# Leaving out the padding columns in layers 2 and 3 of a four-layer graph network

## The chip, the cores and the metric

The kernel runs on one core of one Trainium2 chip. The metric is the device time of one execution in microseconds. Before the change the median of three runs is 1538.35 us (1538.09 to 1540.38).

## The reference

A graph of 3125 nodes with 128 features each and 103,125 directed edges (100,000 drawn, 3125 loops) goes through four graph layers, each with a residual and a layer norm. The change touches the third and the fourth, called layer 2 and layer 3 (counting from 0):

```python
# layer 2: attention along the edges
e = jnp.sum(Q[receiver] * K[sender], axis=-1) * scale
w = jnp.exp(e - m[receiver])
denom = jax.ops.segment_sum(w, receiver, num_segments=num_nodes)
numer = jax.ops.segment_sum(w[:, None] * V[sender], receiver, num_segments=num_nodes)
return x + attn @ Wo           # attn = numer / denom

# layer 3: two rounds of "mean over the neighbours, then two matrices"
x = _sage_conv(features, src, dst, w1_l, b1, w1_r)
x = jax.nn.relu(x)
x = _sage_conv(x, src, dst, w2_l, b2, w2_r)
return jax.nn.sigmoid(x)
```

## The kernel before, in words

**Tiling.** Nodes come in NB = 25 blocks of P = 128, so NP = 3200 columns stand for N = 3125 nodes; the last 75 columns are padding. The edges are turned once, at the start, into a dense matrix of edge counts (bf16, in HBM, `f_ctd`): 25 blocks of 128 sources by 3200 targets. All later layers are dense products against it. A padding node has no edges, so its counts are zero.

**Layer 2** (L1339 to L1448) takes the targets in two groups, `QG`: 13 blocks (1664 columns) and 12 blocks (1536 columns). For each group it walks the 25 source blocks; a pair (group, source block) is an item. `scores` (L1364) loads the item's counts (`ct2`, L1368), and for chunks of m columns multiplies the turned features `xT` with `yT` into a PSUM bank `s` (L1373), takes the exponential on ScalarE (L1376) and multiplies by the counts on VectorE (L1377), which leaves the edge weights in the tile `e2`. m is 416 in the first group (four chunks) and 512 in the second (three). `products2` (L1381) then uses each 128-column block of `e2` as weights and streams 129 columns of values and ones, adding up over the source blocks in PSUM. In program order the scores of item i+1 stand before the products of item i; `ct2` and `e2` have three buffers each, the banks `s` three. `turned_y` (L1345) makes `yT` in steps of 512 columns; the three steps for the second group are put between items near the end of the first (L1423).

**Layer 3** (L1451 on) starts with `add1` (L1473): for each of 25 source blocks, and for each bank of at most 512 columns in `CH` (six of 512 and one of 128), three bf16 parts of the features (`ips`) are the weights and the counts `ct3` are streamed, summing in seven PSUM banks. The last five source blocks are kept and added bank by bank, and in that loop (L1529) each finished bank is scaled by the degrees (`aT`, L1534), goes through the hidden layer (`hidden`, L1505 to L1507, f32 products of the bank's width, Relu into `uT`), and then block by block through `around` and `own` (both by `second`, L1513), which read `uT` in blocks of 128 columns as weights. The second aggregation, `add2` (L1549), uses the counts as weights.

**What orders the work.** [...] Inside layer 2 the order of the item loop is written out in the source. The framework that builds the program adds the waits and may put independent instructions of an engine in another order than the source's: in layer 3 some products of L1549 stand between those of L1513. GpSimd has no work in the second group and in layer 3.

Of the kernel before, what the change touches and what calls it, by code (L numbers as in the profile page):

```python
# [7 lines left out]
F32 = mybir.dt.float32  # L8
# [7 lines left out]
P = 128  # L16
N = 3125
NB = 25
NP = NB * P
# [7 lines left out]
CH = [(c, min(512, NP - c)) for c in range(0, NP, 512)]  # L27
# [472 lines left out]
GM = 40.0  # L500
IG = [(0, 4), (4, 7), (11, 7), (18, 7)]
QG = [(0, 13), (13, 12)]


@with_exitstack
def fast_path(
# [4 lines left out]
    nc = tc.nc  # L511
# [3 lines left out]
    ctd = dram.tile([NB, P, NP], BF16, name="f_ctd")  # L515
# [13 lines left out]
    def copy(o, i):  # L529
        rr[0] ^= 1  # L530
        if rr[0]:
            nc.scalar.copy(o, i)
        else:
            nc.vector.tensor_copy(o, i)
# [317 lines left out]
    for b in range(NBT):  # L852
# [5 lines left out]
        for k in range(0, BW, 4):  # L858
            cp = cps.tile([P, 4, P], F32, name="cp", tag="cw")
            wp = cps.tile([P, 4, P], F32, name="wp", tag="cw")  # L860
            for j in range(4):
                for q in range(2):
                    w = q * BW + k + j
# [4 lines left out]
            for j in range(4):  # L868
                for q in range(2):
                    w = q * BW + k + j  # L870
# [5 lines left out]
            i0 = (b % SB) * BW * WN + k * WN  # L876
# [9 lines left out]
        if b % SB == SB - 1:  # L886
            i0 = (b - SB + 1) * BW * WN
# [30 lines left out]
    nq = lp.tile([P, NB], F32, name="nq")  # L918
    nm = lp.tile([P, len(QG)], F32, name="f_nm")
    due = []  # L920
# [7 lines left out]
    def step():  # L928

        todo = [f for k, f in due if k <= now[0]]  # L930
        due[:] = [(k, f) for k, f in due if k > now[0]]
        for f in todo:
            f()
        now[0] += 1

    def bank():
        return spare[-1]()
# [56 lines left out]
    def bound2(sp, q):  # L994

        i0, n = QG[q]
        mq = sp.tile([P, 1], F32, name="mq")
# [11 lines left out]
    def finish1(sp, g, gap):  # L1009
# [26 lines left out]
        def turns(j):  # L1036
# [5 lines left out]
            else:  # L1042
                nc.gpsimd.tensor_tensor(xs, xs, xs, OP.add)
                for q, (a, m) in enumerate(QG):
                    if i0 < a + m <= i0 + n:
# [4 lines left out]
    with ExitStack() as st:  # L1050
# [238 lines left out]
        acc = None  # L1289
        for x_, (g, hp, c) in enumerate(items):  # L1290
            i0, n = IG[g]
            if (g, hp, c) == (1, 0, 0):
                zero.close()
                ap = st.enter_context(tc.tile_pool(name="f_ap1", bufs=1, space=PSUM))
                spare.append(lambda: ap.tile([P, 512], F32, name="few"))
            if c == 0:
                if g == 0:
                    acc = [zps.tile([P, 512], F32, name="acc1", tag=f"acc{3 + k}") for k in range(2)]
                    acc += [zpp.tile([P, 512], F32, name="acc1", tag=f"left{k}") for k in range(2)]
                else:  # L1300
                    acc = [ap.tile([P, 512], F32, name=f"acc1_{k}") for k in range(n)]
# [32 lines left out]
    with ExitStack() as st:  # L1334
# [4 lines left out]
        ap = st.enter_context(tc.tile_pool(name="f_ap2", bufs=1, space=PSUM))  # L1339
# [3 lines left out]
        def turned_y(a, n):  # L1343
            t = bank()
            nc.tensor.matmul(t[:, :n], wyv[:, 0:P], xT[:, a : a + n], start=True, stop=True)  # L1345
            copy(yT[:, a : a + n], t[:, :n])
# [12 lines left out]

        items = [(q, c) for q in range(len(QG)) for c in range(NB)]  # L1360
        es = {}
        split = QG[1][0] * P

        def scores(q, c):  # L1364
            i0, n = QG[q]
            w = n * P
            ct = cp.tile([P, 13 * P], BF16, name="ct2")
            nc.sync.dma_start(ct[:, :w], ctd[c, :, i0 * P : (i0 + n) * P])  # L1368
            e = cp.tile([P, 13 * P], F32, name="e2")
            m = 416 if w % 416 == 0 else 512  # L1370
            for a in range(0, w, m):
                s = ss.tile([P, 512], F32, name="s")
                nc.tensor.matmul(  # L1373
                    s[:, :m], xT[:, c * P : (c + 1) * P], yT[:, i0 * P + a : i0 * P + a + m], start=True, stop=True
                )
                nc.scalar.activation(e[:, a : a + m], s[:, :m], AF.Exp, bias=nm[:, q : q + 1], scale=scale)  # L1376
                nc.vector.tensor_tensor(e[:, a : a + m], e[:, a : a + m], ct[:, a : a + m], OP.mult)  # L1377
            es[q, c] = e
# [31 lines left out]
        for a in range(0, split, 512):  # L1410
            turned_y(a, min(512, split - a))
        scores(*items[0])
        acc = None
        for x_, (q, c) in enumerate(items):
            i0, n = QG[q]
            if c == 0:
                acc = [ap.tile([P, 512], F32, name=f"acc2_{k}") for k in range((n + 2) // 3)]
            step()
            if (q, c) == (0, 3):
                degrees()  # L1420
            if q == 0 and NB - 4 <= c < NB - 1:
                a = split + (c - NB + 4) * 512
                turned_y(a, min(512, NP - a))  # L1423
            if x_ + 1 < len(items):
                scores(*items[x_ + 1])
            if c < NB - 2:
                for k in range(n):
                    products2(acc, q, c, k)
            elif c == NB - 1:
                for k0 in range(0, n, 3):  # L1430
                    m = min(3, n - k0)
                    for b in (NB - 2, NB - 1):
                        for k in range(k0, k0 + m):
                            products2(acc, q, b, k)
                for k0 in range(0, n, 3):
                    m = min(3, n - k0)
                    t = acc[k0 // 3][:, 0 : m * (P + 1)].rearrange("p (b d) -> p b d", d=P + 1)
                    z = cp.tile([P, 3], F32, name="z2")
                    nc.vector.tensor_scalar(z[:, 0:m], t[:, :, P], 1e-38, None, OP.max)
                    nc.vector.reciprocal(z[:, 0:m], z[:, 0:m])  # L1440
                    for j in range(m):
                        b = i0 + k0 + j
                        nc.vector.scalar_tensor_tensor(
                            r[:, b, :], t[:, j, 0:P], z[:, j : j + 1], x[:, b, :], OP.mult, OP.add
                        )
                finish2(q)
# [5 lines left out]
    with ExitStack() as st:  # L1452
# [4 lines left out]
        ap = st.enter_context(tc.tile_pool(name="f_ap3", bufs=1, space=PSUM))  # L1457
        aT = fp.tile([P, NP], F32, name="f_aT")
        uT = fp.tile([P, 2, NP], F32, name="f_uT")
        v = vo[:, :, 0:P]  # L1460
        for g in range(3, len(GB)):
            b0, n = GB[g]
            ips[g] = in_parts(lp, g, x[:, b0 : b0 + n, :])

        def counts(b):
            ct = cp.tile([P, NP], BF16, name="ct3")
            nc.sync.dma_start(ct, ctd[b])
            return ct


        acc = [ap.tile([P, 512], F32, name=f"acc3_{k}") for k in range(len(CH))]

        def add1(ct, b, k):  # L1473
            c, n = CH[k]
            for s in range(3):
                nc.tensor.matmul(  # L1476
                    acc[k][:, :n], ips[b // 4][:, b % 4, s, :], ct[:, c : c + n], start=(b == 0 and s == 0),
                    stop=(b == NB - 1 and s == 2),
                )

        for b in range(NB - HB):
            ct = counts(b)
            for k in range(len(CH)):
                add1(ct, b, k)
            if 3 <= b < 17 and b % 2:
                turned(ps, xT, *GB[(b - 3) // 2])
            if b == 18:

                sd = fp.tile([P, 1], F32, name="f_sumdeg")
                nc.vector.tensor_reduce(sd, deg, AX.X, OP.add)  # L1490
                t = ps.tile([P, 512], F32, name="tr")
                nc.tensor.matmul(t[:, 0:1], ones, sd, start=True, stop=True)
                nc.vector.tensor_scalar(good[:, 2:3], t[:, 0:1], float(E), None, OP.is_equal)
                nc.vector.tensor_tensor(good[:, 3:4], good[:, 0:1], good[:, 1:2], OP.mult)
                nc.vector.tensor_tensor(good[:, 3:4], good[:, 3:4], good[:, 2:3], OP.mult)
                nc.vector.tensor_copy(flag, good[0:1, 3:4])
# [2 lines left out]

        def hidden(k):  # L1500

            c, n = CH[k]
            for f in range(2):
                t = ap.tile([P, 512], F32, name=f"acc3_{k}") if f == 0 else ps.tile([P, 512], F32, name="tr")
                nc.tensor.matmul(t[:, :n], w1l[:, f * P : (f + 1) * P], aT[:, c : c + n], start=True, stop=False)  # L1505
                nc.tensor.matmul(t[:, :n], w1r[:, f * P : (f + 1) * P], xT[:, c : c + n], start=False, stop=True)
                nc.scalar.activation(uT[:, f, c : c + n], t[:, :n], AF.Relu, bias=b1[:, f : f + 1])  # L1507
# [17 lines left out]
            t = second(ps.tile([P, 512], F32, name="tr"), g, w2r)  # L1525
            nc.vector.tensor_tensor(v[:, b0 : b0 + n, :], t, b2[:, None, :].to_broadcast([P, n, P]), OP.add)

        K = len(CH)
        for k in range(K + 3):  # L1529
            if k < K:  # L1530
                for b in range(NB - HB, NB):
                    add1(last[b], b, k)
                c, n = CH[k]
                nc.vector.tensor_tensor(aT[:, c : c + n], acc[k][:, :n], rdr[:, c : c + n], OP.mult)  # L1534
            if 0 <= k - 1 < K:
                hidden(k - 1)
            if 0 <= k - 2 < K:
                around(k - 2)
            if 0 <= k - 3 < K:
                own(k - 3)  # L1540


        acc = [ap.tile([P, 4, P], F32, name=f"acc3_{g}") for g in range(len(GB))]
# [11 lines left out]
        for b in range(NB - HB):  # L1555
            ct = counts(b)
# [3 lines left out]
        for g, (b0, n) in enumerate(GB):  # L1560
# [10 lines left out]
            m = min(n, NF - b0)  # L1571
# [48 lines left out]
```

## Time and profile before

The execution that was profiled took 1536.56 us.

| | us |
|---|---|
| median of three runs | 1538.35 |
| profiled execution | 1536.56 |
| its span, first to last instruction | 1534.5 |
| TensorE busy in the span | 1400.5 |
| layer 2, second group (25 items) | about 1120 to 1255 |
| layer 3, first aggregation and hidden layer | 1261.7 to about 1412 |
| layer 3, second aggregation on TensorE | 1412.6 to 1505.2 |

In the costliest groups of the page, each line gives the source line, engine and operation, the tiles and shapes, the count, then busy time and mean ns of one, then the idle time before it:

```profile
L1377 DVE TENSOR_TENSOR e<-e,ct 128x416 f32<-128x416 f32 (+1 forms) x175 | 110.4, 636 | 108.2 <-ACT e L1376 102.6
L1376 ACT ACTIVATE e<-s,f_nm 128x416 f32<-128x416 f32 (+1 forms) x175 | 111.5, 642 | 99.4 <-PE s L1373 94.1
L1373 PE MATMUL s<-yT,f_xT 128*128 128x416 f32 (+1 forms) x350 | 145.8, 552 | 4.6 <-ACT rt L1356 4.0
L1381 PE MATMUL acc<-self__8127,e 128*128 128x129 f32 x1250 | 148.7, 276 | 0.6 <-DVE e L1377 0.6
L1476 PE MATMUL acc<-ct,ip 128*128 128x512 bf16 (+1 forms) x525 | 104.9, 360 | 1.4 <-DMA ct<-f_ctd 1.4
```

An f32 product is recorded as two matmuls. A matmul's record begins before its predecessor ends, since they are pipelined; the mean of one (552 ns) is therefore longer than the step from one to the next. The step is read from the chain of waits, where each piece covers only the time that it adds.

### The profile page before, as it was taken

The numbers are of one execution on the slowest core, as the hardware profiler recorded it, in microseconds if no ns is written. First come the engines' busy times: TensorE is split into PE (matmuls) and PEld (weight loads), VectorE is DVE, ScalarE is ACT, GpSimd is POOL, SyncE is SP. The second block draws the span as 40 slices with busy tenths as digits, with TensorE's granted clock in tenths as the row PEclk, the third lists the DMA queues.
The fourth block names the chain that finished last, engine by engine and source line by source line (L and its number), as shares of the span: only waits on it lengthen the run. The fifth ranks groups of instructions, "written<-read, shape, count | busy, mean of one in ns | idle before, by whom it ended". The sixth has DMA issues, their size and how long they took to land.

```text
span 1534.5 us, 35155 instructions
## 1 busy us (share of the span) xinstructions
PE 1400.5 (91%) x14871; PEld 1223.6 (80%) x14871; DVE 981.0 (64%) x1574; ACT 923.4 (60%) x1880; POOL 122.5 (8%) x136
## 2 busy tenths in 40 slices
PE   4899999999997978899989989899999989999995
PEld 3898999998997867899979889577777764458995
DVE  4999899989991389778878887544464360012005
ACT  2988778888882489878778676544474340023006
POOL 1000000000000023203311320300000000000000
PEclk9999999999999999999999999999999999999998
DMA  6387787878877623444434333332222226513551
GB/s 192 91 220 207 203 234 206 235 202 223 214 214 232 222 85 101 143 118 125 132 115 134 114 87 95 106 94 68 67 72 73 82 105 238 193 44 129 195 195 45
DMA packets 210368, 224.39 MB, mean 146 GB/s; under 512 B 72892, under 2 KB 184007, under 8 KB 209945
## 3 DMA queue, kind: packets, MB, share of 16 engines
q1 hardware_dynamic: 206344, 217.74, 48.4%
q10 hardware_dynamic: 3457, 2.35, 0.6%
q8 instruction: 118, 1.93, 0.5%
q0 software_dynamic: 400, 1.97, 0.4%
q14 instruction: 49, 0.40, 0.1%
HBM read 157.67 MB, written 64.36 MB: 145 GB/s over the span
## 4 chain that ended last, share of the span: by engine, by line
PE 40%; DVE 5%; ACT 2%; issue 1%; POOL 1%; DMA 1%; DVEq 0%; ACTq 0%; SPq 0%; POOLq 0%
PE acc L1381 9%; PE s L1373 8%; PE acc L1476 7%; PE acc L1549 6%; PE acc L1241 4%; PE acc L1236 2%; DVE cm L1226 1%; DVE nz L1260 1%; PE tr L1513 1%; PE acc L1513 1%; DMA ct<-f_ctd 1%; ACT fm L1225 1%; DVE cm L1219 0%; PE tr L1505 0%; PE acc L1505 0%
## 5 line engine op out<-in xcount | busy, mean ns | idle before, releaser
L1241 PE MATMUL acc<-vp,cm 128*128 128x198 bf16 x2500 | 344.7, 252 | 6.6 <-DVE cm L1226 4.1
L1225 ACT ACTIVATE fm<-adr,bas 128x896 bf16<-128x896 f32 (+1 forms) x320 | 286.5, 952 | 68.0 <-DVE cm L1226 63.1
L1236 PE MATMUL acc<-vp,ct 128*128 128x204 bf16 x1250 | 315.2, 256 | 10.0 <-DVE vp L1144 5.6
L1241 PEld LDWEIGHTS <-cm 128*128 128x128 bf16 x2500 | 236.0, 98 | 26.5 <-issue 10.6
L872 PE MATMUL wp<-wod,ohc 128*128 128x128 bf16 x3840 | 244.0, 219 | 8.8 <-ACT cs L877 6.6
L872 PEld LDWEIGHTS <-ohc 128*128 128x128 bf16 x3840 | 224.0, 98 | 9.8 <-issue 9.4
L833 DVE TENSOR_TENSOR wod<-ohd,w 128x4096 bf16<-128x4096 bf16 (+1 forms) x120 | 225.0, 1931 | 0.6 <-PE wp L872 0.6
L1226 DVE TENSOR_TENSOR cm<-fm,ct 128x896 bf16<-128x896 bf16 (+1 forms) x320 | 198.1, 649 | 36.1 <-PE acc L1241 14.1
L842 ACT ACTIVATE wod<-ohd,wu 128x128 bf16<-128x128 bf16 x640 | 197.0, 400 | 0.0
L1377 DVE TENSOR_TENSOR e<-e,ct 128x416 f32<-128x416 f32 (+1 forms) x175 | 110.4, 636 | 108.2 <-ACT e L1376 102.6
L1376 ACT ACTIVATE e<-s,f_nm 128x416 f32<-128x416 f32 (+1 forms) x175 | 111.5, 642 | 99.4 <-PE s L1373 94.1
L1381 PEld LDWEIGHTS acc<-self__8127,e 128*128 128x128 f32 x1250 | 148.4, 193 | 21.5 <-issue 19.7
L1373 PE MATMUL s<-yT,f_xT 128*128 128x416 f32 (+1 forms) x350 | 145.8, 552 | 4.6 <-ACT rt L1356 4.0
L1381 PE MATMUL acc<-self__8127,e 128*128 128x129 f32 x1250 | 148.7, 276 | 0.6 <-DVE e L1377 0.6
L794 PE MATMUL acc<-f_xw,cw 128*128 128x128 f32 x1000 | 118.4, 278 | 7.4 <-DMA cw<-wd 7.4
L1236 PEld LDWEIGHTS <-ct 128*128 128x128 bf16 x1250 | 122.4, 98 | 2.5 <-issue 1.5
L883 ACT COPY ws<-wp 128x512 f32<-128x512 f32 x160 | 93.6, 585 | 49.8 <-PE wp L872 48.2
L794 PEld LDWEIGHTS acc<-f_xw,cw 128*128 128x128 f32 x1000 | 115.0, 194 | 7.6 <-DMA cw<-wd 7.6
L864 PE MATMUL cp<-ohc,ohd 128*128 128x125 bf16 x1280 | 96.7, 218 | 21.1 <-ACT ws L883 17.9
L1373 PEld LDWEIGHTS s<-yT,f_xT 128*128 128x128 f32 x350 | 62.2, 191 | 57.7 <-issue 40.6
L1476 PE MATMUL acc<-ct,ip 128*128 128x512 bf16 (+1 forms) x525 | 104.9, 360 | 1.4 <-DMA ct<-f_ctd 1.4
L1549 PE MATMUL acc<-ip,ct 128*128 128x128 bf16 x1875 | 105.2, 219 | 0.0
(277 smaller groups left out, 1482.7 us busy)
## 6 DMA issues: line engine op xcount, KB each, us to landing
ct<-f_ctd SPq DMA_DIRECT2D x50, 800.0 KB
wd<-ws SPq DMA_DIRECT2D x40, 896.0 KB
ct<-f_ctd SPq DMA_DIRECT2D x150, 224.0 KB
cw<-wd SPq DMA_DIRECT2D x50, 640.0 KB
f_ctd<-cs SPq DMA_DIRECT2D x20, 1000.0 KB
ct<-f_ctd SPq DMA_DIRECT2D x25, 416.0 KB
ct<-f_ctd SPq DMA_DIRECT2D x25, 384.0 KB
cw<-wd SPq DMA_DIRECT2D x25, 320.0 KB
```

The lines of the kernel that those rows point to most:

```text
L794: nc.tensor.matmul(accs[j // 4][:, j % 4, :], cw[:, j - h, :], xw[:, i, :], start=False, stop=(i == NB - 1 and (j % 4 == 3 or j == n - 1)) ...
L833: nc.vector.tensor_tensor(f[:, 0:n].rearrange("p w (a t) -> p w a t", t=2), ohd[:, 0:n].rearrange("p w (a t) -> p w a t", t=2), twos(w2[s] ...
L842: nc.scalar.activation(wod[2][:, BW + w, :], ohd[:, BW + w, :], AF.Copy, scale=w3[:, 1, at : at + 1])
L872: nc.tensor.matmul(wp[:, j, :], ohc[:, w, :], wod[s][:, w, :], start=(j == 0 and q == 0 and s == 0), stop=(j == 3 and q == 1 and s == 2), ...
L1225: nc.scalar.activation(f[:, : n * P], at, AF.Relu, bias=bas[:, c, h : h + 1], scale=UP)
L1226: nc.vector.tensor_tensor(m[:, : n * P], f[:, : n * P], ct[:, : n * P], OP.min)
L1236: nc.tensor.matmul(out_(F1, PW), ct[:, k * P : (k + 1) * P], vp[:, c, hp : hp + 2, :, 2 * F1 : V1], start=(c == 0), stop=False, skip_group ...
L1241: nc.tensor.matmul(out_(0, 2 * F1)[:, j], ms[j][:, k * P : (k + 1) * P], vp[:, c, hp + j, :, 0 : 2 * F1], start=False, stop=(c == NB - 1 a ...
L1373: nc.tensor.matmul(s[:, :m], xT[:, c * P : (c + 1) * P], yT[:, i0 * P + a : i0 * P + a + m], start=True, stop=True)
L1381: nc.tensor.matmul(acc[k // 3][:, (k % 3) * (P + 1) : (k % 3 + 1) * (P + 1)], es[q, c][:, k * P : (k + 1) * P], vo[:, c, 0 : P + 1], start ...
L1476: nc.tensor.matmul(acc[k][:, :n], ips[b // 4][:, b % 4, s, :], ct[:, c : c + n], start=(b == 0 and s == 0), stop=(b == NB - 1 and s == 2),)
L1549: nc.tensor.matmul(acc[g][:, j, :], ct[:, (b0 + j) * P : (b0 + j + 1) * P], ups[b // 4][:, b % 4, s, :], start=(b == 0 and s == 0 and j == ...
```

## The change

```diff
+LN = N - (NB - 1) * P
+CN = [(c, min(512, N - c)) for c in range(0, N, 512)]
...
         def scores(q, c):
             i0, n = QG[q]
-            w = n * P
+            w = min(n * P, N - i0 * P)
             ct = cp.tile([P, 13 * P], BF16, name="ct2")
-            nc.sync.dma_start(ct[:, :w], ctd[c, :, i0 * P : (i0 + n) * P])
+            nc.sync.dma_start(ct[:, :w], ctd[c, :, i0 * P : i0 * P + w])
             e = cp.tile([P, 13 * P], F32, name="e2")
-            m = 416 if w % 416 == 0 else 512
+            m = w // (4 if q == 0 else 3)
+            assert w % m == 0 and m <= 512
+            if w < n * P:
+                nc.gpsimd.memset(e[:, w : n * P], 0.0)
             for a in range(0, w, m):
...
-                turned_y(a, min(512, NP - a))
+                turned_y(a, min(512, N - a))
...
         uT = fp.tile([P, 2, NP], F32, name="f_uT")
+        nc.gpsimd.memset(uT[:, :, N:], 0.0)
...
-        acc = [ap.tile([P, 512], F32, name=f"acc3_{k}") for k in range(len(CH))]
+        acc = [ap.tile([P, 512], F32, name=f"acc3_{k}") for k in range(len(CN))]
...
         def add1(ct, b, k):
-            c, n = CH[k]
+            c, n = CN[k]
...
         def hidden(k):
-            c, n = CH[k]
+            c, n = CN[k]
...
-        K = len(CH)
+        K = len(CN)
...
-                c, n = CH[k]
+                c, n = CN[k]
                 nc.vector.tensor_tensor(aT[:, c : c + n], acc[k][:, :n], rdr[:, c : c + n], OP.mult)
```

The second group of layer 2 has w = 1461 columns in place of 1536, in three chunks of 487. The 75 columns of `e2` that `products2` still reads as weights are set to zero on GpSimd, in each of the 25 items. The last step of `turned_y` makes 437 columns. In layer 3 `CN` has the same six banks of 512 and a last one of 53, used by `add1`, the scaling and `hidden`; the 75 padding columns of `uT` are set to zero once. Everything that works in blocks of 128 nodes (`products2`, `around`, `own`, `add2`) keeps its shapes, as does the first group of layer 2.

More of the change, by code (lines that the diff above doesn't have):

```diff
@@ L1482, in fast_path @@
             ct = counts(b)
-            for k in range(len(CH)):
+            for k in range(len(CN)):
                 add1(ct, b, k)
```

## The prediction

> **What bounds the kernel now.** I read the page's chain of waits first, then the same chain in order of time in layers 2 and 3, and then stretches with busy times. The chain's shares say that TensorE leads, and that the two lines of layer 2, L1381 and L1373, lead it.
>
> ```profile
> PE 40%; DVE 5%; ACT 2%; issue 1%; POOL 1%; DMA 1%; DVEq 0%; ACTq 0%; SPq 0%; POOLq 0%
> ```
>
> In order of time (start, length, what) the first group alternates between products of 416 columns (eight records an item: each f32 product leaves two) and the second between products of 512 (six records).
>
> ```profile
> 1089.44 2.79 PE s L1373 x8
> 1092.24 2.90 PE acc L1381 x26
> ...
> 1220.90 2.58 PE s L1373 x6
> 1223.48 2.68 PE acc L1381 x24
> 1226.16 2.58 PE s L1373 x6
> 1228.73 2.68 PE acc L1381 x24
> ```
>
> An item of the second group takes 1226.16 - 1220.90 = 5.26 us, all of it TensorE, with no wait between. The stretches (busy time of PE, PEld, DVE, ACT, POOL, then PEclk, DMA share, GB/s) confirm it:
>
> ```profile
> 1112.00:1250.00 138.00, 138.00 (x787) 100.29 (x786) 66.39 (x143) 69.16 (x109) 0.00 (x0) 1.00 0.23 69
> 1262.00:1350.00 88.00, 88.00 (x456) 42.57 (x455) 7.39 (x20) 6.35 (x13) 0.00 (x0) 0.98 0.63 225
> 1350.00:1413.00 63.00, 63.00 (x378) 42.70 (x377) 17.02 (x28) 21.86 (x36) 0.00 (x0) 1.00 0.17 66
> ```
>
> TensorE is busy for the whole of all three, at the full clock; VectorE, ScalarE and the DMA engines are at half or less, GpSimd does nothing. So a column not streamed through TensorE comes off the end, unless something other than columns sets the pace.
>
> **What the Trainium skill says.** "TensorE: Matmul & The Clock Gate", section "Back-to-back issue gap", gives N/2.4 + 2.5 ns per warm product of N columns, and a floor of some 25 ns for N up to 64. The trace agrees with the first: 128 columns bf16 in layer 3's second aggregation run at 92.64/1659 = 55.8 ns, 55.8 by the formula. No run here shows the floor yet. The same page, section "Weight-path perf modes", says that 128-column weights that aren't f32 are loaded faster. The trace's weight loads (min/median/max ns) fit that:
>
> ```profile
> L1091 PEld LDWEIGHTS tr_ad<-f_xT,watt x14: 82/84/86, 502.1 to 562.5; 128*4 128x4 f32 x14
> L1381 PEld LDWEIGHTS acc<-self__8127,e x1250: 186/192/338, 971.4 to 1254.7; 128*128 128x128 f32 x179
> L1476 PEld LDWEIGHTS <-ip x525: 95/98/181, 1261.6 to 1396.3; 128*128 128x128 bf16 x175
> ```
>
> Four f32 columns take 84 ns and 128 take 192, so (192-84)/124 = 0.87 ns a column over a fixed 80 ns; 128 bf16 columns take 98, only some 18 over it, if the fixed part is the same. "SBUF — State Buffer", section "Who interferes with whom", lets a VectorE instruction with two SBUF inputs collide with GpSimd only where that one reads SBUF; a memset only writes. The trace of before shows no such pair. That page's "Specifications (TRN2)" speaks of lines of 16 bytes and a penalty for each crossing to a new one, without a price; no product of the trace of before is known to pay it, and this is the open point below.
>
> **The change part by part.**
>
> *Score products.* The price of a column is read from the two groups: 2.58/6 = 0.430 us a record at 512 columns, 2.79/8 = 0.349 at 416, so 0.081/96 = 0.846 ns a column and record. Each record of the second group loses 25 columns: 21.1 ns. There are 25 items x 6 = 150: **-3.17 us**, all on the chain. ScalarE (688 ns at 512, 607 at 416) and VectorE (692 and 594) also lose some 20 to 25 ns an instruction. That is worth nothing: three of each make 2.1 us of a 5.26 us item. Widths and starts become odd (columns 487 and 974, bytes 1948 and 3896). Odd width is shown harmless: the 129-column products take 2.68/24 = 111.7 ns a record, the 128-column f32 ones 1.79/16 = 111.9. A moving operand that starts off a 16-byte boundary isn't shown. I take 0; below nothing is excluded, since no column is saved twice.
>
> *Which chunk a block needs.* Block k=3 (columns 384 to 511) now spans chunks one and two, k=7 chunks two and three. Scores run a whole item ahead of their products, so the later chunk has 2.5 us or more after its multiply. Item 24 is products-only with item 23's between; its groups of three need the same chunks as before. Cost 0.
>
> *The memset of 75 columns, 25 times.* It is not in the old trace; GpSimd's memsets took 113 ns for 7 f32 columns and 195 for 128, so about 155 ns here. It waits for the products of three items back and is needed by the last block, over 10 us later. GpSimd has nothing else in this stretch, so nothing queues behind it. What it adds is a wait on TensorE at k=11. Waits that are met cost nothing that shows: 26 records with four chunk waits take 111.5 ns each, 24 with three 111.7. A separate semaphore instruction took 51 ns on the weight queue where there was one; 25 of them uncovered would be 1.3 us. I take 0. The memset of uT runs once at layer 3's start, some 90 us before its use: 0.
>
> *The count load* shrinks from 384 KB to 365 KB, in rows of 2922 bytes. The queue alternates between busy and quiet slices here (23% in all), and three buffers hold it. 0 either way, even if odd rows took twice as long. No DMA is moved.
>
> *turned_y*: the last call streams 437 columns for 512, two records on the chain (0.86 us): 150 x 0.846 = **-0.13 us**.
>
> *Last bank of the first aggregation.* 25 blocks x 3 products go from 128 to 53 columns. Their pace now is 0.84/15 = 56 ns. Three follow each other with three different weights, so the loads could set the pace. The one place with few columns after a full load is the f32 product of 8 columns (L1087), eight records from 512.58 to the next instruction's 513.57:
>
> ```profile
> 512.58 0.97 PEld L1087 LDWEIGHTS tr_sa<-watt,f_xT 128*128 128x128 f32 x8
> 513.57 0.09 PEld L1091 LDWEIGHTS tr_ad<-f_xT,watt 128*4 128x4 f32 x2
> ```
>
> That is 124 ns a record, slower than 128 columns at 112: few f32 columns are paced by the load, 128 x 0.87 = 111 plus about 13. With bf16's estimated 18 ns the same sum is 31, rounded up to 34 for the guess in it; saved 22 ns x 75 = **-1.65 us**. Bounds: the skill's floor of 25 saves 31 x 75 = 2.3; a load like f32's, half of 124 = 62, loses 6 x 75 = 0.45. Count loads aren't next in line: 800 KB at 225 GB/s take 3.6 us, a block still lasts about 3.98 of 4.05, and six buffers are ahead.
>
> *hidden(6).* Eight f32 records go from 128 to 53 columns and become load-paced: 8 x 12 ns = **+0.10 us**. Its two Relus (368 ns) and the multiply of aT (284) shorten by 60 to 80 ns, but TensorE is what the chain shows here. around and own read all 128 columns as before.
>
> The sum: -3.17 - 0.13 - 1.65 + 0.10 = **-4.85 us**. The profiled execution took 1536.56 us with a span of 1534.5, so 1531.7 and 1529.7. The median of the runs shown is 1538.35, 1.8 above the profiled execution; the same saving gives **1533.5 us**.
>
> **The rivals.** A measurement of this kernel can tell 0.2%, or 3.1 us, from no change.
>
> 1. *The sum holds*, last bank included: -3.8 to -5.6, 1533.5. For it: the price per column comes from the same line in the same layer. Chance 0.62.
> 2. *Only layer 2 pays*: the load sets the last bank's pace and eats it. -3.2 to -2.75, about 1535.2. For it: the f32 case of 8 columns. Against it: 98 beside 192 ns. Chance 0.20, split evenly by the bound.
> 3. *Part of the columns' gain is eaten* by odd starts or by the wait at k=11: 25 x 51 ns and 100 records x 15 to 20 ns take about 3 us, leaving -1.6: 1536.8. For it: the old trace has no such starts. Against it: met waits are free. Chance 0.10.
> 4. *Slower.* Moving operands that start off a 16-byte boundary stream at a lower rate. Two of three chunks do, so 100 records. A quarter more on 409 ns is 102 ns, 10.2 us in all, net +5.4: 1543.7. It decides from 4.85/100 = 49 ns a record on, and is slower by over 0.2% from 79 ns. Against it: the products' PSUM outputs at steps of 129 f32 already start oddly at no cost, though that is the other side of TensorE. Chance 0.08.
>
> **How the numbers follow.** The first case gives faster 0.60 and same 0.02, the second 0.11 and 0.09, the third same 0.10, the fourth slower 0.08: faster 0.71, same 0.21, slower 0.08. The range takes in cases 1 and 2 and some of 3: -5.6 gives 1532.7, -2.75 gives 1535.6, and the three runs of before lie 2.3 apart, so 1531.5 to 1536.5.
>
> **What would show it.** In the chain, second-group scores at 2.45 us an item for 2.58 and the item at 5.13; all three chunks alike (case 4 shows chunks two and three longer than the first). L1381's 24 records still at 2.68; at 2.73 or more the wait at k=11 costs. Fifteen last-bank records at 0.5 us for 0.84 (case 2: at 0.84). Layer 3 from 1261 to 1395 shorter by about 1.3 us beyond what layer 2 shifts it. The memsets near 155 ns, 25 of them, and no wait of TensorE on GpSimd. I am wrong if the score records don't fall by 21 ns each, or if the gap of about 6 us between layers 2 and 3 grows.

## The result, and the profile after

| | before | after |
|---|---|---|
| median of five runs, us | 1538.20 (1535.90 to 1540.38) | 1529.79 (1528.91 to 1532.03) |
| ratio | 1 | 0.9952, 95% interval 0.9941 to 0.9964 |
| span of the profiled execution, us | 1534.5 | 1527.5 |

By the ratio, the change is faster by 7.4 us (5.5 to 9.1 by the interval); the two medians lie 8.4 us apart, since the ratio is not their quotient. Both are more than the 4.85 us that the sum gave, and 1529.79 lies below the range of 1531.5 to 1536.5. L1373 of before is L1378 after, L1381 is L1386, L1476 is L1482, L1513 is L1519 and L1549 is L1555.

The chain of waits after the change, in order of time (start, length, what), from the first regular item of layer 2 (the first whose eight score records stand together) to the second aggregation:

```profile
997.04 2.79 PE s L1378 x8
...
1222.32 2.45 PE s L1378 x6
1224.77 2.68 PE acc L1386 x24
1227.45 2.46 PE s L1378 x6
...
1257.22 33.33 PE acc L1482 x168
1291.04 7.92 PE acc L1482 x42
...
1389.44 0.38 PE acc L1482 x15
...
1396.91 0.16 PE acc L1511 x2
...
1397.29 0.73 PE acc L1519 x6
...
1405.71 92.64 PE acc L1555 x1659
```

An item takes 1227.45 - 1222.32 = 5.13 us for 5.26; the scores are 2.46 for 2.58 and the products unchanged at 2.68. The last bank's fifteen products in the final loop take 0.38 us. The same view of the kernel before:

```profile
998.32 2.79 PE s L1373 x8
...
1322.00 8.10 PE acc L1476 x42
...
1395.71 0.84 PE acc L1476 x15
...
1404.50 0.38 PE tr L1505 x2
...
1412.56 92.64 PE acc L1549 x1659
```

So a product of 53 columns takes 0.38/15 = 25 ns where 34 had been assumed, and two source blocks 7.92 us for 8.10.

The hidden layer's f32 products on the last bank did not become faster, although the chain gives their first pair 0.16 us where it was 0.22: the six products behind them take 0.73 us, 0.06 more than six at the usual 112 ns, so that one piece pays back what the other gained. The weight loads in the timeline (start, length, engine) show the pace, after the change and then before:

```profile
1397.75 0.30 PEld L1511 LDWEIGHTS tr<-f_aT,f_w1l 128*128 128x128 f32 x2
1397.98 0.30 PEld L1512 LDWEIGHTS tr<-f_xT,f_w1r 128*128 128x128 f32 x2
```

```profile
1403.34 0.30 PEld L1505 LDWEIGHTS acc<-f_aT,f_w1l 128*128 128x128 f32 x2
1403.56 0.30 PEld L1506 LDWEIGHTS acc<-f_xT,f_w1r 128*128 128x128 f32 x2
```

Two loads follow each other in 0.22 to 0.23 us at 53 columns as at 128, that is 111 to 112 ns a record in both. What this stretch did gain, 0.15 us, is a wait that went away. Before, the pair of L1505 at 1404.50 in the chain took 0.38 us for 0.22: it writes the bank `tr`, which VectorE reads (L1526) until 1404.33, 0.06 us before the pair's first record. After, two more products of `around` stand ahead of the pair, and the bank is free in time.

The timeline of one item after the change (in brackets the idle time before, and what ended it) shows the records of the three chunks by their weight loads, each of which starts with the record before it:

```profile
1222.56 0.19 PEld L1378 LDWEIGHTS s<-yT,f_xT 128*128 128x128 f32 x1 [0.22 <-issue]
1222.97 0.19 PEld L1378 LDWEIGHTS s<-yT,f_xT 128*128 128x128 f32 x1 [0.22 <-issue]
1223.38 0.19 PEld L1378 LDWEIGHTS s<-yT,f_xT 128*128 128x128 f32 x1 [0.22 <-issue]
1223.79 0.19 PEld L1378 LDWEIGHTS s<-yT,f_xT 128*128 128x128 f32 x1 [0.22 <-issue]
1224.20 0.19 PEld L1386 LDWEIGHTS acc<-self__8127,e 128*128 128x128 f32 x1 [0.22 <-issue]
```

The steps are all 0.41 us. Chunks two and three, which start 1948 and 3896 bytes behind the first, are as fast as it: the odd starts cost nothing. The memset takes 0.16 us, and no wait of TensorE on GpSimd shows in layer 2.

These stages don't explain all. From the first regular item of layer 2's first group (998.32 before, 997.04 after) to the start of the second aggregation (1412.56, 1405.71), before takes 414.24 us and after 408.67: 5.57 us less. Another 1.28 us of the span's 7.0 had gone before layer 2 began, where the two programs give every engine the same instructions in the same order; 0.15 went at the end. The experiments had to settle whether that 1.28 belongs to the change.

### The profile page after: what moved, and what is told of

Its sections match the earlier page's. It is cut to its first block, busy times and chain, and to the rows that moved or that the text cites. A ratio compares the mean times of both kernels' runs of the same rounds, so it can differ in the third digit from the quotient of the medians.

```text
span 1527.5 us, 35222 instructions
## 1 busy us (share of the span) xinstructions
PE 1395.1 (91%) x14871; PEld 1220.8 (80%) x14871; DVE 978.3 (64%) x1574; ACT 921.5 (60%) x1880; POOL 127.8 (8%) x162
## 5 line engine op out<-in xcount | busy, mean ns | idle before, releaser
L1381 ACT ACTIVATE e<-s,f_nm 128x416 f32<-128x416 f32 (+1 forms) x175 | 109.6, 633 | 97.8 <-PE s L1378 90.8
L1386 PEld LDWEIGHTS acc<-self__8127,e 128*128 128x128 f32 x1250 | 148.2, 193 | 20.6 <-issue 18.8
L1386 PE MATMUL acc<-self__8127,e 128*128 128x129 f32 x1250 | 148.6, 276 | 0.6 <-DVE e L1382 0.6
L1378 PE MATMUL s<-yT,f_xT 128*128 128x416 f32 (+1 forms) x350 | 142.8, 543 | 4.6 <-ACT rt L1358 4.0
L866 PE MATMUL cp<-ohc,ohd 128*128 128x125 bf16 x1280 | 96.7, 218 | 21.1 <-ACT ws L885 17.9
L1378 PEld LDWEIGHTS s<-yT,f_xT 128*128 128x128 f32 x350 | 62.1, 191 | 55.5 <-issue 39.2
L1555 PE MATMUL acc<-ip,ct 128*128 128x128 bf16 x1875 | 105.2, 219 | 0.0
L826 DVE TENSOR_TENSOR ohd<-kd,ramp 128x4096 bf16<-128x4096 bf16 x40 | 91.5, 2288 | 21.2 <-PE cp L866 21.1
```

The costliest lines, as they stand in the source:

```text
L1378: nc.tensor.matmul(s[:, :m], xT[:, c * P : (c + 1) * P], yT[:, i0 * P + a : i0 * P + a + m], start=True, stop=True)
L1386: nc.tensor.matmul(acc[k // 3][:, (k % 3) * (P + 1) : (k % 3 + 1) * (P + 1)], es[q, c][:, k * P : (k + 1) * P], vo[:, c, 0 : P + 1], start ...
L1555: nc.tensor.matmul(acc[g][:, j, :], ct[:, (b0 + j) * P : (b0 + j + 1) * P], ups[b // 4][:, b % 4, s, :], start=(b == 0 and s == 0 and j == ...
```

## The experiments

Theory A: columns set TensorE's pace, both parts pay what their stages show, and the rest is the spread of the layers before. Theory B: the change somehow also makes the earlier layers faster. Theory L, for the last bank: weight loads set its pace. The diffs stand against the changed kernel, E4's against the kernel before.

**E1: layer 2's part alone.** Layer 3 keeps its bank of 128 and the change's memset of `uT` is gone.

```diff
-        nc.gpsimd.memset(uT[:, :, N:], 0.0)
-        acc = [ap.tile([P, 512], F32, name=f"acc3_{k}") for k in range(len(CN))]
+        acc = [ap.tile([P, 512], F32, name=f"acc3_{k}") for k in range(len(CH))]
...
-        K = len(CN)
+        K = len(CH)
```

> Layer 2's part alone (three score products of 487 columns, the memset, the shorter turned_y); layer 3 keeps its bank of 128. Theory A (columns alone set the pace, the rest of the measured gain is the spread of the layers before): the item of the second group lasts 5.13 us for 5.26, 3.2 to 3.3 us in all, layer 3's first aggregation is unchanged (168 products in 34.3 us), ratio about 0.998. Theory B (the change also makes layers 0 and 1 faster, by where the program lies): layer 2's first group starts over 1 us earlier than in the kernel before, in this run too, and the ratio is nearer 0.997.

**E2: layer 3's part alone.** `scores` and `turned_y` are those of before.

```diff
-            w = min(n * P, N - i0 * P)
+            w = n * P
...
-            m = w // (4 if q == 0 else 3)
+            m = 416 if w % 416 == 0 else 512
```

> Layer 3's part alone (last bank of 53 columns in the first aggregation, the scaling and the hidden layer; memset of uT); layer 2 keeps 1536 columns. Theory A: the 75 products of the last bank go from 56 to 25 ns, 2.3 us, and the tail gains about 0.1 more: ratio about 0.9984. Theory L (the weight loads set the pace at 34 ns or more): 1.6 us or less, two source blocks in 7.97 us or more for 8.10 before. Theory B: over 1 us more than that, from before layer 2.

**E3: the whole change once more.**

> The whole change once more. Theory A: what its stages show, 5.5 to 5.8 us (ratio 0.9963), with the start of layer 2's first group within 1 us of the kernel before on average; the 7.4 us measured first was partly spread. Theory B: 7 us or more again, with layer 2 starting over 1 us earlier again.

**E4: nothing changed** but two unused constants.

```diff
 QG = [(0, 13), (13, 12)]
+LN = N - (NB - 1) * P
+CN = [(c, min(512, N - c)) for c in range(0, N, 512)]
```

> The kernel before with two unused constants added, so that nothing of the program changes but line numbers. Every theory: ratio 1.000; how far its interval and the start of layer 2 in its profile lie from the kernel before is the spread that the other runs are to be judged by. If it is 0.1% or more off, differences of 1 to 2 us between kernels say nothing.

Measured together, against 36 runs of the kernel before with a median of 1535.85 us. The last three columns are from the profiles: where the first regular item of layer 2 and the second aggregation begin, and the time between.

| kernel | median, us | ratio (95% interval) | layer 2 begins | second aggregation | between |
|---|---|---|---|---|---|
| before | 1535.85 | 1 | 998.32 | 1412.56 | 414.24 |
| E4, nothing | 1535.99 | 1.0000 (0.9992 to 1.0008) | 997.41 | 1411.55 | 414.14 |
| E1, layer 2 alone | 1532.20 | 0.9976 (0.9968 to 0.9984) | 997.23 | 1408.10 | 410.87 |
| E2, layer 3 alone | 1533.42 | 0.9989 (0.9980 to 0.9999) | 996.92 | 1408.88 | 411.96 |
| E3, the change again | 1530.52 | 0.9967 (0.9955 to 0.9980) | 997.86 | 1406.52 | 408.66 |
| the change, first profile | 1529.79 | 0.9952 (0.9941 to 0.9964) | 997.04 | 1405.71 | 408.67 |

The lines of E1's and E2's chain of waits that the verdict rests on:

```profile
1113.92 5.25 PE s L1378 x14
...
1317.54 8.11 PE acc L1481 x42
```

```profile
1113.74 5.37 PE s L1375 x14
...
1319.39 7.92 PE acc L1479 x42
```

E1 has the short scores (5.25 for the fourteen records around the group's start) and the old last bank (8.11 for two source blocks), E2 the reverse (5.37 and 7.92). Against the unchanged E4, E1 saves 414.14 - 410.87 = 3.27 us, E2 2.18, the whole change 5.48. That the two parts add up to within 0.03 us is in part luck, as the same time in three stretches shows: layer 2 up to the first product of layer 3, the first eight source blocks of layer 3, and from there to the second aggregation.

| kernel | layer 2, us | eight source blocks, us | clock in their first 10 us | the rest, us |
|---|---|---|---|---|
| before | 263.33 | 34.26 | 0.83 | 116.65 |
| E4, nothing | 263.17 | 34.32 | 0.82 | 116.65 |
| E1, layer 2 alone | 260.16 | 34.07 | 0.85 | 116.64 |
| E2, layer 3 alone | 263.26 | 33.55 | 0.83 | 115.15 |
| E3, the change again | 260.13 | 33.38 | 0.84 | 115.15 |
| the change, first profile | 260.18 | 33.34 | 0.85 | 115.15 |
| E7 (below), same layer 3 | 260.32 | 33.83 | 0.80 | 115.15 |

On average layer 2 gains 3.05 us and the rest of layer 3 1.50 us where the change's part is in, and neither moves by more than 0.2 us where it isn't. The stretch between them also follows the clock that TensorE was granted. Its first 10 us in the view of stretches, the change and then E7 (busy time of the five engines, then the granted clock as a share of full speed, DMA share and GB/s):

```profile
1257.22:1267.22 10.00, 10.00 (x45) 4.36 (x46) 5.48 (x14) 5.45 (x11) 0.22 (x1) 0.85 1.02 423
1258.54:1268.54 10.00, 10.00 (x43) 4.26 (x44) 5.33 (x14) 5.31 (x11) 0.22 (x1) 0.80 1.01 413
```

The work is the same in both, the clock is (0.85 - 0.80) x 10 = 0.5 us of full speed lower in E7, and E7 takes 0.49 us longer. With each kernel's own loss taken off ((1 - clock) x 10 us), the eight blocks take 32.5 to 32.6 us with the bank of 128 and 31.8 to 31.9 with that of 53, 0.7 less; 24 products at 31 ns are 0.74. So the change is worth 3.05 + 0.7 + 1.50 = 5.3 us at an equal clock. E1's 3.27 holds 0.25 us from these eight blocks, which E1 leaves alone, and the 5.48 holds some 0.2.

The start of layer 2 lies between 996.92 and 998.32 in the six profiles of the first table, in no order that goes with the change; E4, which changes nothing, came 0.91 us earlier than before. E7 and E8, which contain the whole change, start it at 998.22 and 998.87. Theory B falls. The whole change's ratio, taken again beside 36 runs of before, is 5.1 us (3.1 to 6.9), and its first ratio of 7.4 us contains about 2 us that aren't the change's. Of E1's and E2's ratios alone, 3.7 us (2.5 to 4.9) and 1.7 (0.2 to 3.1), neither could have told 5.3 from 4.85; the stages can.

**E5 and E6: the last bank at other widths.** At 16 columns the first aggregation and the hidden layer leave out the last 37 nodes; at 96, 43 of the padding columns are in again.

```diff
-CN = [(c, min(512, N - c)) for c in range(0, N, 512)]
+LB = 16
+CN = [(c, 512) for c in range(0, 3072, 512)] + [(3072, LB)]
...
-        nc.gpsimd.memset(uT[:, :, N:], 0.0)
+        nc.gpsimd.memset(uT[:, :, 3072 + LB :], 0.0)
```

E6 has `LB = 96`.

> The change with a last bank of 16 columns: the first aggregation and the hidden layer leave out the last 37 nodes. Fifteen products of the last bank in the final loop took 0.38 us at 53 columns and 0.84 at 128. Theory C (columns set the pace, by the formula N/2.4 + 2.5): 9 ns a product, 0.14 us for fifteen. Theory L (at 53 something fixed, a load or an issue floor, already sets the pace): 0.38 again. Between them the value is the floor. Saved against the change: 75 products x 16 ns, 1.2 us, under C; 0 under L.

> The change with a last bank of 96 columns, 43 of the padding columns left in. Theory C: 96/2.4 + 2.5 = 42.5 ns a product, 0.64 us for fifteen, 1.3 us more in 75 than with 53. Theory L with a load over 25 ns: a pace that doesn't lie on that line.

The fifteen last-bank products in the chain of waits of E5, then of E6:

```profile
1389.56 0.36 PE acc L1483 x15
```

```profile
1392.07 0.64 PE acc L1483 x15
```

A product takes 24 ns at 16 columns, 25 at 53, 43 at 96 and 56 at 128; from record to record it is 25 ns at 16 columns too. The formula that the prediction took from the Trainium skill ("TensorE: Matmul & The Clock Gate", section "Back-to-back issue gap"), N/2.4 + 2.5, gives 9, 24.6, 42.5 and 55.8. So columns set the pace down to 53, and below that a floor of 25 ns does, as that section says; 53 columns sit where the two meet. E5 by itself came out as theory L said (0.36 us, where L expected 0.38 and C 0.14), and saved nothing: 408.73 us between the marks. But a load that took longer than 25 ns would show at 53, and none does: theory L falls for this bank of bf16. What makes the floor, the load of new weights or the issue of a product, isn't told apart, since every product here has its own weights. The same section expects some 81 ns for a product of 128 columns in a stream of loads and products; the 55.8 measured here, with a load before each product, decides against that.

For the f32 products of the hidden layer theory L holds. Their loads follow each other in 0.22 to 0.23 us for two at 16 columns (E5), 53 and 96 (E6) as at 128, that is 111 to 112 ns a record at every width.

**E7 and E8: the cover of the memset.** The memset of the 75 columns is written 20 and 40 times in each item.

```diff
-                nc.gpsimd.memset(e[:, w : n * P], 0.0)
+                for _ in range(20):
+                    nc.gpsimd.memset(e[:, w : n * P], 0.0)
```

> The change with the zeroing of the 75 columns written 20 times over in each item: 20 x 161 ns is 3.2 us of GpSimd in an item of 5.13 us. If the three buffers hide the memset: the item stays at 5.13 us and no wait on GpSimd shows. If the wait at the last block has little cover: TensorE waits in each item, up to 3 us x 25.

> The same 40 times over: 6.4 us of GpSimd an item, more than TensorE's 5.13. GpSimd becomes the bound of the second group: items of 6.4 us after the first ones, up to 25 x 1.3 = 33 us more in all, less what the buffers hold ahead (25 to 33). If the cover were one item or less, 20 times would already have cost, and this more.

E7, GpSimd's timeline in one item:

```profile
1192.76 4.31 POOL L1376 MEMSET e<- 128x75 f32 x20 [0.82 <-PE acc L1387]
```

GpSimd starts when the products of three items back have released the buffer and works for 4.31 us, 216 ns a memset, and the item still lasts 5.13 to 5.14 us. TensorE nowhere waits for it. E7 took 409.30 us between the two marks, 0.63 more than the change, of which 0.49 is the clock at the start of layer 3. VectorE's multiply, which reads two tiles, took 667 ns beside twenty memsets as beside one.

E8, GpSimd's timeline for 24 of the 25 items:

```profile
1126.45 162.57 POOL L1376 MEMSET e<- 128x75 f32 x960 [2.91 <-PE acc L1387]
```

Here GpSimd is the bound: it works without a break for 162.57/24 = 6.8 us an item, or 169 ns a memset. TensorE waits for it 18 times, 32.3 us in all, in most items before the last block's two records. The span grew to 1567.8 us, and 446.61 us lie between the marks, 37.9 more than in the change. That is above the 25 to 33 expected, which had 161 ns a memset. So 4.31 us of GpSimd's work an item are covered and 6.8 are not; where between them the cover ends wasn't tried.

## Why the prediction was right and wrong

**The bound: right.** TensorE sets the end in both layers, and what ScalarE, VectorE and the loads save is worth nothing. It was not at the full clock in all three stretches, as the prediction read its own lines (the second has 0.98): layer 3 starts at a lower clock, and how long this lasts made 0.5 us between the change and E7.

**Scores and turned_y: right, and a little high.** 3.30 us were reckoned together, and layer 2 shows 3.05. The item went from 5.255 us ((1220.90 - 1126.31)/18) to 5.134 ((1222.32 - 1124.78)/19), so a record lost 20.2 ns, not 21.1.

**Chunk boundaries, memset, the wait at k=11, count load: right at 0.** The 24 products stay at 2.68 us, E7 shows the memset's cover, no new wait stands in the list, and the gap between layers 2 and 3 did not grow (9.21 us in the chain before, 9.22 after).

**The step that failed: 13 ns put on top of the weight load in the last bank.** The prediction read L1087, eight f32 records of 8 columns, as 124 ns a record: a load of 111 and "about 13". It had divided 0.99 us by eight, and the 0.99 reach to the start of the next instruction. One by one, these records start 111 to 112 ns apart after a first step of 133, and the last step, to L1091, is 184. So few f32 columns run at the load's own 111, as do 128 columns and the hidden layer's 53, and the 13 doesn't exist. The same 13 went into the next sentence: "With bf16's estimated 18 ns the same sum is 31, rounded up to 34". Without it 18 is left, which lies under the floor of 25, so the columns' 25 ns hold: 75 x 31 = 2.3 us, the upper bound that the text gave. The last bank and hidden(6) were reckoned at -1.65 + 0.10 = -1.55 us and gave 0.7 + 1.50 = 2.2. In this, the hidden layer's f32 products gave nothing and cost nothing: that the load paces them was right, that it costs more than 128 columns was not. The wait that went away gave 0.15 us, which the prediction didn't have. Some 0.03 us is lost wherever f32 products follow the short bf16 ones (four transposes take 0.48 us for 0.44).

So the sum was 0.65 us too low in layer 3 and 0.25 too high in layer 2: 4.85 for 5.3.

**The time itself** missed by more than that. The sum was set against a median of three runs, 1538.35. Over 36 later runs the same kernel has 1535.85, so the base was 2.5 us high, and the first five runs of the change lie a little lower than those of E3 (1529.79 and 1530.52, within their scatter). From 1535.85 the forecast's 4.85 would have given 1531.0 and the stages' 5.3 gives 1530.6, beside E3's 1530.52. The range allowed for the spread of three runs, but not for a base that was itself off by more than the runs' half width. Chance alone doesn't explain that base well: four of the first five runs of before lie above 1538 us, and only four of the 36. What was different then isn't known.

**The rivals.** The first holds. The second (the load sets the last bank's pace) falls by E5 and E6, the third and fourth (odd starts, the wait at k=11) by the even steps of 0.41 us and E7. The proof given for odd widths, 129 columns as fast as 128, shows nothing, since both run at the load's pace; the 0.41 us at 487 columns shows it.

## What to carry to other kernels

Where TensorE is busy without a gap, the value of narrower products is columns times the price per column from two widths of the same line; here it came within a tenth, 3.05 us for 3.30. Ask first whether columns set the pace. In this kernel bf16 products with new weights each time cost only their columns down to 53. F32 products with new 128-column f32 weights each time took 111 to 112 ns at 8, 16, 53, 96, 128 and 129 columns; at 0.846 ns a column, columns would set their pace only from about 132 on (an estimate from these two figures).

Take the price of one record from the steps between like records, and not from the first start to the next instruction. Next to a switch between kinds of products, a piece of the chain can gain what its neighbour loses, so add up the whole stretch. Judge effects of a few microseconds by marks that enclose the change, split at the places where the clock changes, and leave the absolute time of a program with a noisy first part to many runs of both kernels.

## What the runs showed that was not expected

- The floor of 25 ns, which the prediction had only as a bound, holds for bf16 products with a new load of 128-column weights before each (16 columns), and 53 columns just reach it.
- The f32 products of the hidden layer take as long at 16 columns as at 128.
- A moving f32 operand that starts 12 or 8 bytes past a multiple of 16, counted from the first chunk, streams at the full rate: 0.41 us a record at 487 columns for all three chunks. The penalty for crossing lines of 16 bytes, which the prediction took from the Trainium skill ("SBUF — State Buffer", section "Specifications (TRN2)"), doesn't show in it.
- The last stretch of the table repeats to 0.01 us between profiles, while the eight blocks before it vary by 0.5 us with the granted clock, and what comes before layer 2 by 1.95 us (996.92 to 998.87) in programs that are the same up to there.
